# The last stage of a 384-channel attention and binarized-convolution kernel: a written engine order, other queues and 18-partition moves

## Chip, cores and metric

One core of one Trainium2 chip runs the kernel. The metric is device time in microseconds (us) of one execution. The engines are TensorE (PE; its weight loads are PEld), VectorE (DVE), ScalarE (ACT), GpSimd (POOL) and SyncE (SP). DMAs are issued from the queues of SP, ACT and POOL and run on 16 DMA engines.

## The reference

The input x is 1 x 384 x 192 x 192 in float32. Two residual layers follow each other (cut to what matters here):

```python
x = x + L0(gn(x))   # layer 0: channel attention
x = x + L1(gn(x))   # layer 1: binarized 1x1 convolution with shifts

# L0, its end: out is at half resolution
out = gelu(out)
out = repeat(repeat(out, 2, axis=2), 2, axis=3)
out = einsum('bchw,oc->bohw', out, w_proj) + b_proj

# L1
xb = sign(x); wb = sign(weight)
dx = (arange(C) + 3) % 7 - 3          # -3 .. 3, by channel
shifted[:, c, :, w] = xb[:, c, :, w + dx[c]]   # zero outside the row
out = einsum('bchw,oc->bohw', shifted, wb) + bias
```

Only the sign of the normalized x enters layer 1, so its normalization needs the group means and no variance: the kernel takes sign(x - mean).

## The kernel before

The image is cut into 24 units of 8 rows. One unit of x is a tile `xt` of 128 partitions x 3 x 1536 float32 (2304 KB); channel c of the 384 lies at a partition p and a third t that the table `XCH` of `shift_blocks` (L65) gives. Stages 1 to 4 read x for the statistics, for queries and keys, and for the values. At the end of stage 4 the attention output lies in six tiles `chunk`, four units each, in the pool `big`, which has eight buffers; the other two still hold the last two units of x. A short step (L456 to L476) works out `nmean1`, the group means of layer 1.

The **last stage** (L481 to L550) does the rest, unit by unit, from the last unit to the first. For each unit:

- x is in a kept buffer or is loaded (`unit`, L112; L495) through POOL's queue.
- Nine float32 matmuls of 384 columns, each two instructions (L501), give the projection `yps`; six DVE instructions of 768 elements (L510) add it to both rows of each pair in `xt`.
- Three ACT instructions (L516) write the signs as fp8 into one of two tiles `signs`, with rows at a pitch of 196, four of them zero, so that a shift of up to three columns reads zeros beyond a row.
- 14 DMAs through SP's queue (L526) copy the signs to one of two tiles `moved`, each channel shifted by its own dx. Seven of them move 16 partitions with all three thirds (4700 bytes of each partition); six move 7 partitions of one third; one moves 2 partitions.
- 27 fp8 matmuls of 512 columns (L534), in blocks of 4 x 128 or 8 x 64 pixels, give the convolution `l1ps`, one PSUM bank for each block; nine DVE instructions of 512 elements (L542) add it and the bias to `xt`.
- `xt` is stored through POOL's queue (L550).

The order of the instructions on each engine is worked out by the framework's scheduler from dependencies and its own estimates. A buffer for a load comes from `big` or from the pool `more` of two. After every fourth unit a `chunk` has been used up, and its buffer becomes one more for loads. On POOL's queue a load that waits for its buffer stands ahead of later stores.

The functions that the change touches:

Of the kernel before, what the change touches and what calls it, by code (L numbers as in the profile page):

```python
# [10 lines left out]
F32 = mybir.dt.float32  # L11
F8 = mybir.dt.float8e4
AF = mybir.ActivationFunctionType
ALU = mybir.AluOpType
AX = mybir.AxisListType
PSUM = bass.MemoryType.PSUM

P = 128
C = 384
CT = C // P  # L20
# [7 lines left out]
UR = 8  # L28
NU = H // UR
# [2 lines left out]
PPX = PR * WP  # L32
KS = (HD // 2, HD * 2 // 3, HD * 3 // 4, HD * 4 // 5)
SHIFT = 7
SP = 16
PITCH = W + 4
LEAD = 4
SLEN = UR * PITCH
ABLK = 512
NAB = NPX // ABLK  # L40
UC = 4
CR = UC * PR
CPX = CR * WP
NCH = NU // UC
NST = NU * (UPX // 512) * 6
NBIG = 8
MORE = 2
KEEP = 6
RESIDENT = NBIG - NCH
TOPK = 1  # L50
NSIGNS = 2


BLOCKS = ((0, 4, 0, 128), (4, 4, 0, 128), (0, 8, 128, 64))
# [10 lines left out]
def shift_blocks():  # L65

    left = [list(range(s, C, SHIFT)) for s in range(SHIFT)]
    at = np.full((P, CT), -1)  # L70
    blocks = []

    def put(s, p0, n, t0, nt):
        for t in range(t0, t0 + nt):
            for p in range(p0, p0 + n):
                at[p, t] = left[s].pop(0)
        blocks.append((p0, n, t0, nt, (s + SHIFT // 2) % SHIFT - SHIFT // 2))

    for s in range(SHIFT):
        put(s, SP * s, SP, 0, CT)  # L80
    rest = SP * SHIFT
    n = len(left[0])
    for s in range(2 * CT):
        put(s, rest + (s % 2) * n, n, s // 2, 1)
    put(SHIFT - 1, rest + 2 * n, P - rest - 2 * n, 0, CT)
    assert not any(left) and (at >= 0).all()
    return at, blocks


XCH, SHIFTS = shift_blocks()  # L90


@with_exitstack
def conv_preact_kernel(ctx: ExitStack, tc: tile.TileContext, a: dict, out: bass.AP):
    nc = tc.nc
    xv = a["x"].rearrange("u p (t n) -> u p t n", n=UPX)
    ov = out.rearrange("u p (t n) -> u p t n", n=UPX)
# [4 lines left out]
    big = ctx.enter_context(tc.tile_pool(name="big", bufs=NBIG))  # L102
# [4 lines left out]
    bl1 = const.tile([P, CT], F32, name="bl1")  # L107
    nmean0 = const.tile([P, CT], F32, name="nmean0")
    nmean1 = const.tile([P, CT], F32, name="nmean1")
    wb = const.tile([P, CT, C], F8, name="wb")  # L110

    def unit(u, pool=big, queue=nc.sync):  # L112
        xt = pool.tile([P, CT, UPX], F32, name="xt", tag="big")
        queue.dma_start(xt, xv[u])  # L114
        return xt

    def inv_sqrt(pool, y, s, n, tag):
# [43 lines left out]
    kept = {}  # L161
    with tc.tile_pool(name="p1", bufs=1, side="right") as p1, tc.tile_pool(name="p1ps", bufs=2, space=PSUM) as psp:
        stats = p1.tile([P, CT, NST], F32, name="stats0")
        grp = p1.tile([P, CT, C], F32, name="grp_s0")
        for u in reversed(range(NU)):
            xt = unit(u)
# [14 lines left out]
            for t in range(CT):  # L181
                for j in range(UPX // 512):
                    i = (u * (UPX // 512) + j) * 6
# [20 lines left out]
        ps = psp.tile([P, NM], F32, name="bqps")  # L204
        for m in range(NM):
            for t in range(CT):
# [4 lines left out]
                    start=(t == 0),  # L211
                    stop=(t == CT - 1),
# [3 lines left out]
    def padded(pool, n):  # L216


        ts = []
        for m in range(n):  # L220
            t = pool.tile([P, PR + 3, WP + 2], F32, name=f"pooled{m}")
            nc.gpsimd.memset(t, 0.0)
            ts.append(t)
        return ts
# [41 lines left out]
    with tc.tile_pool(name="p2w", bufs=1, side="right") as wp, tc.tile_pool(  # L266
        name="p2t", bufs=2, side="right"
    ) as tp, tc.tile_pool(name="p2qkv", bufs=3, space=PSUM) as pqkv, tc.tile_pool(
        name="p2tr", bufs=2, space=PSUM
    ) as ptr, tc.tile_pool(name="p2g", bufs=1, space=PSUM) as pg:  # L270
        pool = padded(wp, 2 * CT)
        dwo = [wp.tile([P, (PR + 1) * WP], F32, name=f"dw{m}") for m in range(2 * CT)]
        gram = [pg.tile([P, 512], F32, name=f"gram{t}") for t in range(CT)]
        for u in range(NU):
            xt = kept.pop(u) if u in kept else unit(u)
            lo, hi = rows(u)
            n = hi - lo + 1
# [5 lines left out]
            for c0 in range(0, n * WP, P):  # L283
                L = min(P, n * WP - c0)
                qkT = tp.tile([P, 2, C], F32, name="qkT")
                for s in range(2):
                    ps = ptr.tile([P, C], F32, name="tr")
# [3 lines left out]
                first, last = u == 0 and c0 == 0, u == NU - 1 and c0 + P >= n * WP  # L291
                for t in range(CT):
# [4 lines left out]
                        start=first,  # L297
                        stop=last,
# [98 lines left out]
    with ExitStack() as vs:  # L397
# [4 lines left out]
        psp = vs.enter_context(tc.tile_pool(name="p3ps", bufs=2, space=PSUM))  # L402
        pool = padded(wp, CT)
# [3 lines left out]
        todo, steps = [], None  # L407
# [20 lines left out]
        for u in range(NU):  # L428
            xt = unit(u)
# [6 lines left out]
            last = first + hi - lo  # L436
            for m in range(CT):
                parts = []
                for c in range(first // CR, last // CR + 1):
                    r0, r1 = max(first, c * CR), min(last, c * CR + CR - 1)  # L440
# [15 lines left out]
    with tc.tile_pool(name="p5w", bufs=1, side="right") as wp, tc.tile_pool(name="p5mps", bufs=1, space=PSUM) as psp:  # L456
# [5 lines left out]
        ps = psp.tile([P, CT], F32, name="ymps")  # L462
        for m in range(CT):
            for t in range(CT):
# [4 lines left out]
                    start=(t == 0),  # L469
                    stop=(t == CT - 1),  # L470
# [7 lines left out]
    att.close()  # L478


    with tc.tile_pool(name="p5x", bufs=MORE) as more, tc.tile_pool(name="p5s", bufs=1) as sp, tc.tile_pool(  # L481
        name="p5py", bufs=3, space=PSUM
    ) as pyp, tc.tile_pool(name="p5ps", bufs=5, space=PSUM) as psp:
        signs = [sp.tile([P, LEAD + CT * SLEN + PITCH], F8, name=f"signs{i}") for i in range(NSIGNS)]
        moved = [sp.tile([P, CT * SLEN], F8, name=f"moved{i}") for i in range(2)]
        for t in signs:
            nc.gpsimd.memset(t[:, :LEAD], 0.0)
            nc.gpsimd.memset(t[:, LEAD:].rearrange("p (r w) -> p r w", w=PITCH)[:, :, W:], 0.0)  # L488
        free = [big] * RESIDENT + [more] * MORE
        for i, u in enumerate(u for c in reversed(range(NCH)) for u in reversed(range(c * UC, (c + 1) * UC))):  # L490
            if i and i % UC == 0:
                free.insert(0, big)
            pool = free.pop(0)
            free.append(pool)
            xt = kept.pop(u) if u in kept else unit(u, pool, nc.gpsimd)  # L495
            o = chunk[u // UC][:, :, u % UC * PPX : (u % UC + 1) * PPX]
            x5 = xt.rearrange("p t (i a j b) -> p t a i j b", a=2, b=2, j=WP)
            for m in range(CT):
                ps = pyp.tile([P, PPX], F32, name="yps")
                for t in range(CT):  # L500
                    nc.tensor.matmul(  # L501
                        ps,
                        wpr[:, t, m * P : (m + 1) * P],
                        o[:, t, :],
                        start=(t == 0),
                        stop=(t == CT - 1),
                    )
                yb = ps.rearrange("p (i j) -> p i j", j=WP).unsqueeze(3).to_broadcast([P, PR, WP, 2])
                for r in range(2):
                    nc.vector.scalar_tensor_tensor(  # L510
                        x5[:, m, r], yb, bpr[:, m : m + 1], x5[:, m, r], ALU.add, ALU.add
                    )
            sg, mo = signs[i % NSIGNS], moved[i % 2]
            rows3 = sg[:, LEAD : LEAD + CT * SLEN].rearrange("p (t r w) -> p t r w", r=UR, w=PITCH)
            for t in range(CT):
                nc.scalar.activation(  # L516
                    rows3[:, t, :, :W],
                    xt[:, t, :].rearrange("p (r w) -> p r w", w=W),
                    AF.Sign,
                    bias=nmean1[:, t : t + 1],  # L520
                    saturate=False,
                )
            for p0, n, t0, nt, dx in SHIFTS:
                run = nt * SLEN - (PITCH - W)
                at = t0 * SLEN
                nc.sync.dma_start(  # L526
                    mo[p0 : p0 + n, at : at + run], sg[p0 : p0 + n, LEAD + dx + at : LEAD + dx + at + run]
                )
            x4 = xt.rearrange("p t (r w) -> p t r w", w=W)
            for m in range(CT):  # L530
                for r0, nr, c0, ncol in BLOCKS:
                    ps = psp.tile([P, 512], F32, name="l1ps")
                    for t in range(CT):
                        nc.tensor.matmul(  # L534
                            ps,
                            wb[:, t, m * P : (m + 1) * P],
                            mo[:, t * SLEN : (t + 1) * SLEN].rearrange("p (r w) -> p r w", w=PITCH)[:, r0 : r0 + nr, c0 : c0 + ncol],
                            start=(t == 0),
                            stop=(t == CT - 1),
                        )  # L540
                    blk = x4[:, m, r0 : r0 + nr, c0 : c0 + ncol]
                    nc.vector.scalar_tensor_tensor(  # L542
                        blk,
                        ps.rearrange("p (r w) -> p r w", w=ncol),
                        bl1[:, m : m + 1],
                        blk,
                        ALU.add,
                        ALU.add,
                    )
            nc.gpsimd.dma_start(ov[u], xt)  # L550


# [69 lines left out]
```

## Time and profile before

Three runs took 2556.58, 2549.80 and 2550.52 us, median 2550.52. The profiled execution took 2556.03 us; its span, from the first to the last instruction, is 2554.3 us. All durations below come from that one execution.

| what | us | how to read it |
|---|---|---|
| span | 2554.3 | stages 1 to 4 and the short step until about 2113, the last stage from there |
| PE busy | 2247.0 | 88% of the span, 6235 matmuls |
| DVE busy | 1894.8 | 74% |
| ACT busy | 645.0 | 25% |
| L501 matmuls, yps | 166.9 | 432 instructions |
| L534 matmuls, l1ps | 157.3 | 648 instructions |
| L510 adds | 136.3 | 144 instructions, 1011 ns each in the mean |
| L542 adds | 146.0 | 216 instructions, 744 ns each in the mean |
| L516 signs | 108.6 | 72 instructions, 1566 ns each |
| L526 issues of moves | 336 issues | 0.52 to 2.65 us each in SP's queue, median 0.69 |
| x loads, last stage | 22 | 2304 KB each, 10.0 us from issue to landing (median) |
| stores | 24 | 2304 KB each, 10.2 us (median) |

PE's granted clock was full until the last stage and 0.75 to 0.93 in its stretches of 50 us. The DMA engines' share of time was 0.12 in stage 2 and 0.77 to 0.88 in the middle of the last stage.

### The profile page before, as it was taken

How to read it: one execution, taken by the hardware profiler on the slowest of the kernel's cores; microseconds unless marked ns; L12 is line 12 of the kernel's file. 1: busy time of each engine (PE TensorE's matmuls, PEld its weight loads, DVE VectorE, ACT ScalarE, POOL GpSimd, SP SyncE). 2: the span in 40 equal slices, each digit the busy share in tenths (PEclk: the TensorE clock that was granted, in tenths of full speed). 3: DMA queues.
4: the chain of work that ended last, by engine and by line, in shares of the span. 5: the costliest groups of instructions: out<-in, count | busy, mean ns of one | idle time of the engine just before them, and what ended most of it. 6: DMA issues, size and time to landing. Idle time of an engine off the chain costs nothing. (4 is left out here: it accounts for less than half of the span.)

```text
span 2554.3 us, 18523 instructions
## 1 busy us (share of the span) xinstructions
PE 2247.0 (88%) x6235; PEld 1069.3 (42%) x6235; DVE 1894.8 (74%) x3187; ACT 645.0 (25%) x1282; POOL 34.2 (1%) x67
## 2 busy tenths in 40 slices
PE   0039999999999999999999999999999998687864
PEld 0034444444444444444444444444444444343421
DVE  6956777777777777777778899956668676676763
ACT  0002323332322323232322221232222223222131
POOL 0000000000000000000000000000000000000000
PEclk9999999999999999999999999999999999888987
DMA  9941011100110111100100120211011106888976
GB/s 374 430 205 37 37 38 65 47 37 37 54 58 38 37 42 70 37 1 37 37 38 37 65 111 37 111 74 74 37 75 58 71 29 228 301 306 291 331 245 227
DMA packets 28463, 285.25 MB, mean 112 GB/s; under 512 B 8240, under 2 KB 10784, under 8 KB 13904
## 3 DMA queue, kind: packets, MB, share of 16 engines
q1 hardware_dynamic: 16992, 170.17, 18.0%
q0 software_dynamic: 6624, 108.53, 11.0%
q10 hardware_dynamic: 4752, 5.37, 0.6%
q8 instruction: 49, 0.80, 0.1%
q14 instruction: 46, 0.38, 0.0%
HBM read 212.99 MB, written 56.62 MB: 106 GB/s over the span
## 5 line engine op out<-in xcount | busy, mean ns | idle before, releaser
L238 PE MATMUL qkv<-xt,wq 128*128 128x512 f32 x3888 | 1699.4, 593 | 7.7 <-DVE pooled L245 7.4
L238 PEld LDWEIGHTS qkv<-xt,wq 128*128 128x128 f32 x3888 | 727.3, 190 | 871.4 <-issue 798.7
L261 DVE SCALAR_TENSOR_TENSOR dw<-pooled,wdw,dw 128x384 f32<-128x384 f32 (+2 forms) x1152 | 709.5, 616 | 250.9 <-ACT dw L259 226.9
L245 DVE TENSOR_REDUCE pooled<-qkv 128x128 f32<-128x512 f32 x648 | 443.9, 686 | 141.0 <-PE qkv L238 134.1
L261 DVE SCALAR_TENSOR_TENSOR chunk<-pooled,wdw,chunk 128x384 f32<-128x384 f32 (+3 forms) x696 | 362.6, 548 | 46.2 <-ACT chunk L259 34.7
L263 ACT COPY pooled<-pooled 128x196 f32<-128x196 f32 x207 | 73.7, 356 | 737.8 <-DVE dw L261 520.2
L252 ACT ACTIVATE pooled<-pooled,bq 128x384 f32<-128x384 f32 x216 | 133.1, 616 | 386.7 <-DVE pooled L245 386.7
L501 PE MATMUL yps<-chunk,wpr 128*128 128x384 f32 x432 | 166.9, 545 | 68.8 <-DVE xt L510 68.5
L542 DVE SCALAR_TENSOR_TENSOR xt<-l1ps,bl,xt 128x512 f32<-128x512 f32 x216 | 146.0, 744 | 82.8 <-PE l1ps L534 71.8
L534 PE MATMUL l1ps<-moved,wb 128*128 128x512 fp8e4 x648 | 157.3, 402 | 42.4 <-DMA moved<-signs 35.3
L510 DVE SCALAR_TENSOR_TENSOR xt<-yps,bpr,xt 128x768 f32<-128x768 f32 x144 | 136.3, 1011 | 66.8 <-DMA xt<-in_x_dram 51.6
L516 ACT ACTIVATE signs<-xt,nmean 128x1536 fp8e4<-128x1536 f32 x72 | 108.6, 1566 | 301.2 <-DMA moved<-signs 246.9
L501 PEld LDWEIGHTS yps<-chunk,wpr 128*128 128x128 f32 x432 | 90.7, 214 | 139.2 <-DVE xt L510 59.8
L184 DVE BATCH_NORM_STATS2 stats<-xt 128x6 f32<-128x512 f32 x216 | 130.5, 679 | 24.8 <-DMA xt<-in_x_dram 23.8
L133 PE MATMUL gm_m<-cm,grp_s 128*128 128x1 f32 x18 | 4.0, 353 | 161.5 <-DVE cm L189 161.5
L534 PEld LDWEIGHTS <-wb 128*128 128x128 fp8e4 x648 | 65.5, 102 | 134.7 <-issue 54.6
L282 ACT ACTIVATE sq<-dw 128x384 f32<-128x384 f32 (+2 forms) x144 | 75.2, 522 | 157.8 <-DVE dw L261 157.8
L416 PE MATMUL ops<-chunk,aT 128*128 128x512 f32 x252 | 109.0, 592 | 0.0
L259 ACT ACTIVATE dw<-pooled,bdw,wdw 128x384 f32<-128x384 f32 (+2 forms) x144 | 100.8, 700 | 30.0 <-PE tr L289 28.2
L289 PE MATMUL tr<-ident,dw 128*128 128x128 f32 (+2 forms) x438 | 74.2, 279 | 8.8 <-DVE dw L261 8.0
L289 PEld LDWEIGHTS tr<-ident,dw 128*128 128x128 f32 (+2 forms) x438 | 52.3, 140 | 70.4 <-DVE dw L261 30.9
L293 PEld LDWEIGHTS gram<-qkT 128*128 128x128 f32 (+2 forms) x438 | 64.4, 190 | 25.3 <-ACT qkT L290 19.9
(91 smaller groups left out, 470.9 us busy)
## 6 DMA issues: line engine op xcount, KB each, us to landing
xt<-in_x_dram SPq DMA_DIRECT2D x66, 2304.0 KB
out_dram<-xt POOLq DMA_DIRECT2D x24, 2304.0 KB, 10.2
xt<-in_x_dram POOLq DMA_DIRECT2D x22, 2304.0 KB, 10.0
moved<-signs SPq DMA_DIRECT2D x168, 73.4 KB
moved<-signs SPq DMA_DIRECT2D x144, 10.7 KB
wq<-in_w_qkvT_dram ACTq DMA_DIRECT2D x1, 1728.0 KB
grp_s<-in_grp_dram ACTq DMA_DIRECT2D x2, 576.0 KB
tri<-in_tri_dram ACTq DMA_DIRECT2D x1, 1152.0 KB
```

Source lines behind the costliest of these rows:

```text
L184: nc.vector.bn_stats(stats[:, t, i : i + 6], xt[:, t, j * 512 : (j + 1) * 512])
L238: nc.tensor.matmul(ps, wq[:, t, m * P : (m + 1) * P], x4[:, t, r0 : r0 + nr, c0 : c0 + ncol], start=(t == 0), stop=(t == CT - 1),)
L245: nc.vector.tensor_reduce(pl[:, 2 + r0 // 2 : 2 + (r0 + nr) // 2, 1 + c0 // 2 : 1 + (c0 + ncol) // 2], ps.rearrange("p (i a j b) -> p i j ...
L252: nc.scalar.activation(new, new, AF.Identity, bias=bq[:, m : m + 1])
L261: nc.vector.scalar_tensor_tensor(acc2, src, wdw[:, m, k : k + 1], acc2, ALU.mult, ALU.add)
L289: nc.tensor.transpose(ps[:L, t * P : (t + 1) * P], dwo[s * CT + t][:, c0 : c0 + L], ident)
L416: nc.tensor.matmul(ps, aT[:, k, t * P : (t + 1) * P], chunk[c][:, k, cols], start=(k == MEET[t][0]), stop=(k == MEET[t][-1]),)
L501: nc.tensor.matmul(ps, wpr[:, t, m * P : (m + 1) * P], o[:, t, :], start=(t == 0), stop=(t == CT - 1),)
L510: nc.vector.scalar_tensor_tensor(x5[:, m, r], yb, bpr[:, m : m + 1], x5[:, m, r], ALU.add, ALU.add)
L516: nc.scalar.activation(rows3[:, t, :, :W], xt[:, t, :].rearrange("p (r w) -> p r w", w=W), AF.Sign, bias=nmean1[:, t : t + 1], saturate=False,
L534: nc.tensor.matmul(ps, wb[:, t, m * P : (m + 1) * P], mo[:, t * SLEN : (t + 1) * SLEN].rearrange("p (r w) -> p r w", w=PITCH)[:, r0 : r0 + ...
L542: nc.vector.scalar_tensor_tensor(blk, ps.rearrange("p (r w) -> p r w", w=ncol), bl1[:, m : m + 1], blk, ALU.add, ALU.add,)
```

## The change

`shift_blocks` groups 18 partitions per shift instead of 16: seven blocks of 18 partitions with all three thirds, and two left partitions whose thirds need shifts that step by one from third to third, or no shift. A unit then has seven moves of 18 partitions, issued from ACT's queue right after the signs, and three small moves from POOL's queue. The x loads of the last stage go to SP's queue, which carries nothing else there; the stores stay on POOL's.

The last stage is split into two functions. `signed(i)` does the projection, the adds, the signs and the moves of a unit; the signs of a third now follow its adds at once. `finished(i)` does the convolution, the adds of the convolution and the store. They are called in a fixed order, which each engine follows as written: signed(0), then signed(i+1), finished(i) for each i. Loads are issued where a buffer becomes free: after the store of a unit and after the last use of a chunk.

The convolution is cut into 36 matmuls of 384 columns (two image rows each); two of these groups fill two PSUM banks, and one DVE instruction adds 768 elements over both banks, six per unit. The projection has two PSUM buffers instead of three, the convolution three pairs of banks instead of five banks. The last unit is stored in three parts. The pools of the stage are opened with the option that waits for single tiles of what lay in the space before.

```diff
-SP = 16
+SP = P // SHIFT
@@ shift_blocks
-    for s in range(SHIFT):
-        put(s, SP * s, SP, 0, CT)
-    rest = SP * SHIFT
-    n = len(left[0])
-    for s in range(2 * CT):
-        put(s, rest + (s % 2) * n, n, s // 2, 1)
-    put(SHIFT - 1, rest + 2 * n, P - rest - 2 * n, 0, CT)
+    for i, dx in enumerate(sorted(left)):
+        put(i * SP, SP, 0, CT, dx)
+    put(P - 2, 1, 0, CT, 1, 1)
+    put(P - 1, 1, 0, 2, -3, 1)
+    put(P - 1, 1, 2, 1, 0)
@@ last stage
+        def opened(name, bufs, **kw):
+            return last.enter_context(tc.tile_pool(name=name, bufs=bufs, reuse_waits="tile", **kw))
+        more, sp = opened("p5x", MORE), opened("p5s", 1)
+        pyp, psp = opened("p5py", 2, space=PSUM), opened("p5ps", 3, space=PSUM)
...
-        free = [big] * RESIDENT + [more] * MORE
-        for i, u in enumerate(u for c in reversed(range(NCH)) for u in reversed(range(c * UC, (c + 1) * UC))):
-            if i and i % UC == 0:
-                free.insert(0, big)
-            pool = free.pop(0)
-            free.append(pool)
-            xt = kept.pop(u) if u in kept else unit(u, pool, nc.gpsimd)
+        free = [more] * MORE
+        todo = [u for u in order if u not in kept]
+        home = {u: big for u in kept}
+        def loads():
+            while free and todo:
+                u = todo.pop(0)
+                home[u] = free.pop(0)
+                kept[u] = unit(u, home[u])
+        def signed(i):
...
-            for p0, n, t0, nt, dx in SHIFTS:
-                run = nt * SLEN - (PITCH - W)
-                at = t0 * SLEN
-                nc.sync.dma_start(
-                    mo[p0 : p0 + n, at : at + run], sg[p0 : p0 + n, LEAD + dx + at : LEAD + dx + at + run]
-                )
+            for p0, n, t0, nt, dx, step in SHIFTS:
+                at = LEAD + dx + t0 * SLEN
+                if step or nt < CT:
+                    one = SLEN - (PITCH - W)
+                    src = sg[p0 : p0 + n, at : at + nt * (SLEN + step)]
+                    nc.gpsimd.dma_start(
+                        to[p0 : p0 + n, t0 : t0 + nt, :one],
+                        src.rearrange("p (t n) -> p t n", t=nt)[:, :, :one],
+                    )
+                else:
+                    run = CT * SLEN - (PITCH - W)
+                    nc.scalar.dma_start(
+                        to[p0 : p0 + n].rearrange("p t n -> p (t n)")[:, :run], sg[p0 : p0 + n, at : at + run]
+                    )
+            if i % UC == UC - 1:
+                free.append(big)
+                loads()
+        def finished(i):
...
             for m in range(CT):
-                for r0, nr, c0, ncol in BLOCKS:
-                    ps = psp.tile([P, 512], F32, name="l1ps")
-                    for t in range(CT):
...
-                    blk = x4[:, m, r0 : r0 + nr, c0 : c0 + ncol]
+                for r0 in range(0, UR, 4):
+                    ps = psp.tile([P, 2, 512], F32, name="l1ps")
+                    for j in range(2):
+                        for t in range(CT):
+                            nc.tensor.matmul(
+                                ps[:, j, : 2 * W],
+                                wb[:, t, m * P : (m + 1) * P],
+                                mo[:, t, r0 + 2 * j : r0 + 2 * j + 2, :W],
+                                start=(t == 0),
+                                stop=(t == CT - 1),
+                            )
+                    blk = xt[:, m, r0 * W : (r0 + 4) * W].rearrange("p (j n) -> p j n", j=2)
                     nc.vector.scalar_tensor_tensor(
...
+                        blk, ps[:, :, : 2 * W], bl1[:, m : m + 1], blk, ALU.add, ALU.add
+                    )
+                if i == NU - 1:
+                    nc.gpsimd.dma_start(ov[u, :, m], xt[:, m])
+            if i < NU - 1:
+                nc.gpsimd.dma_start(ov[u], xt)
+            free.append(home[u])
+            loads()
+        with tc.manual_schedule():
+            loads()
+            signed(0)
+            for i in range(NU):
+                if i < NU - 1:
+                    signed(i + 1)
+                finished(i)
```

## The prediction

> **What bounds the kernel now.** I read the table of stretches first, to find the last stage and its engines. The stage starts with the first yps matmul at 2112.9 us and ends with the span, so it is 441 us of 2554.3. The stores are the milestones: the first was issued at 2149.1, the 16th at 2441.7, the 24th at 2544.4. The last x load was issued at 2433.9. That cuts the stage into four: 36 us of start, 15 store intervals of 19.5 us with loads running (292.6 us), 8 intervals of 12.8 us without loads (102.7 us), 9.9 us of end.
>
> ```profile
> 2149.00:2441.00 292.00, 222.52 (x745) 112.11 (x744) 196.70 (x249) 66.16 (x45) 18.06 (x34) 0.87 0.84 306
> 2441.00:2544.00 103.00, 60.85 (x223) 23.81 (x221) 55.31 (x79) 27.05 (x18) 4.26 (x8) 0.78 0.68 226
> ...
> 2262.00:2270.00 8.00, 3.11 (x10) 1.53 (x9) 6.05 (x8) 1.49 (x2) 0.54 (x1) 0.80 1.01 380
> ...
> 2398.00:2406.00 8.00, 7.58 (x33) 3.35 (x31) 6.78 (x10) 0.00 (x0) 0.47 (x1) 1.00 0.99 378
> ```
>
> The columns are PE, PEld, DVE, ACT and POOL busy, then granted clock, DMA share, GB/s. With loads running, PE is busy 76%, DVE 67%, and the DMA engines 84% at 306 GB/s. Seven 8 us stretches in which the share reached 0.97 to 1.04 moved 356 to 401 GB/s, 380 in the mean. So no engine is full, but DMA has only a fifth to give. What keeps them all from being full shows in the waits of that stretch (total us, times, longest) and in the chain of waits (start, us, what).
>
> ```profile
> ACT signs L516 <- DMA moved<-signs: 200.4, 13, 23.5
> POOL xt L114 <- DMA out_dram<-xt: 164.6, 14, 17.5
> ...
> DVE xt L510 <- DMA xt<-in_x_dram: 49.3, 12, 8.2
> ```
>
> ```profile
> 2229.00 10.12 DMA out_dram<-xt
> ...
> 2239.67 9.69 DMA xt<-in_x_dram
> ...
> 2249.48 1.95 DVE xt L510 x2
> ...
> 2264.68 15.67 DMA out_dram<-xt
> ```
>
> The loop is: store, load into its buffer, residual add of that load, PE behind the add (yps waited 68.5 us for L510's buffers), next store. The load issued at 2239.7, when the fifth store had landed, is the eleventh unit's; its add sits in DVE's and PE's order ahead of the l1ps work of the sixth unit. The order runs five units ahead, so finished work waits for a load that waits for a store. The loop takes some 36 to 40 us and passes two units. Without loads the limit is another one: SyncE's queue, which issues moves without a pause. The timeline (start, us, engine, line; in brackets the idle time before and its releaser) has it last, under the prices of a unit's l1ps work on PE and DVE:
>
> ```profile
> 2198.25 5.99 PE L534 MATMUL l1ps<-moved,wb 128*128 128x512 fp8e4 x27
> ...
> 2199.17 6.02 DVE L542 SCALAR_TENSOR_TENSOR xt<-l1ps,bl,xt 128x512 f32<-128x512 f32 x9 [4.87 <-PE l1ps L534]
> ...
> 2440.51 95.14 SPq L526 DMA_DIRECT2D moved<-signs  x98
> ```
>
> 98 issues in 95.1 us, 14 per unit, is 13.6 us per unit against the interval of 12.8 in those units. PE and DVE need 6.0 us each for one unit's l1ps and are idle for the rest.
>
> **The change, step by step.** Call S the work of `signed` and F that of `finished`.
>
> *Prices per unit.* PE: S is unchanged, 18 matmuls in 6.07 us where it runs at full clock (2150.8). F has 36 matmuls of 384 columns for 27 of 512, the same 13,824 columns. No row has an fp8 matmul of 384, so it lies between 5.99 us (by columns) and 8.0 us (36 at the 0.222 us of each of the 27). I take 6.0, because the f32 matmuls of 384 and 512 columns go by columns: 0.337 us (6.07/18) against 0.437 (1699.4/3888). PE is then 12.1 us. DVE: F has six adds of 768 elements instead of nine of 512; at the 0.94 us of L510 (six in 5.64 from 2188.7) that is 5.64 instead of 6.02, so DVE is 11.3 us. The 0.4 us saved is worth nothing, since PE covers it; without that cover it would be 9 us in all. Two yps buffers instead of three cost nothing while DVE empties one (1.9 us) as fast as PE fills the other (2.0); a late DVE would hold PE by 1.9 us per unit. ACT: 4.5 us of signs as now, plus seven issues that were SyncE's. An undisturbed issue took 0.59 us (2482.9); seven under traffic, from 2440.5, took 0.55, 0.90, 0.58, 1.59, 1.40, 1.74 and 2.35, together 9.1. ACT is 8.6 to 13.6 us. Behind a blocked issue stand the next unit's signs, and behind them its moves. POOL: three small moves and a store at 0.53 us, 2.1 us. The small moves stand in POOL's queue behind the store of unit i-1, which took 10 to 16 us to land; F of i+1 needs them an interval and an S later (17 + 6 us by the sum below), so they cost nothing, but a store over 23 us would show. SyncE: loads alone, each waiting only for its buffer; nothing stands behind them but later loads.
>
> *The moves on the DMA engines.* Bytes stay at 0.60 MB per unit, but 18 partitions replace 16. These are the queue totals of the 292 us, and then q1 on the page (packets, MB, share of 16 engines):
>
> ```profile
> q0 software_dynamic: 4874, 80.11, 72.6%
> q1 hardware_dynamic: 4659, 9.01, 11.6%
> ```
>
> ```profile
> q1 hardware_dynamic: 16992, 170.17, 18.0%
> ```
>
> The page's 16,992 packets are 66 loads of 128+16 and 24 units of 7x(16+16) + 6x(7+7) + (2+2): one data packet and one closing packet per partition of a move, so 16 partitions used 16 engines. 18 on 16 engines put two on at least one, so the fullest engine gets 14 big packets per unit where an even spread would give 7.9. A 4.7 KB packet costs 0.28 us (11.6% of 292 x 16 engine-us is 542 for 9.01 MB). The surplus is between 0 (that engine catches up in lulls) and 6.1 x 0.28 = 1.7 us per unit, 26 us over 15 units. The rows do not say which, so I take the middle, 13. The Trainium skill (DMA: Bandwidth & Descriptors, "Why a DMA increments its semaphore by 16 and not by 1") states that a DMA uses the largest number of engines up to 16 that divides the slowest dimension, which for 18 would be nine engines with two each. The counts for 16 and 7 agree with it, no row shows 18; by it the 26 would hold and the end would be 13 us later.
>
> *Start.* The signs of the first unit ended at 2124.4 and still will. Seven issues of 0.59 (4.1) and 2.4 us of landing (2471.9) give 2130.9; F with its last add 6.9. The first store comes at 2138 instead of 2149.1, because F of the first unit no longer stands behind S of the fourth. 11 us gained. The first two loads may now start before 2113.7; I cost that at nothing, since S of the third unit comes only after 2137, when they have landed (10 us) even if issued as now.
>
> *The 15 intervals with loads.* A load now has all the buffers' slack, S is one unit ahead, so the loop above opens and the DMA engines become the bound. Work between first and 16th store, if the loads again run ahead: 15 stores, 20 loads, 15 units of moves, 35 x 2.36 + 9.0 = 91.6 MB. At 380 GB/s that is 241 us, with the surplus 254, 16.9 us per unit. PE (12.1), DVE (11.3) and ACT (13.6 at worst) lie beside it. Bounds: 241 to 267.
>
> *The 8 intervals without loads.* SyncE's 13.6 us of issues are gone; PE's 12.1 is next, 97 us instead of 102.7. DMA needs 5.3 us for a store (2.36 MB at the 442 GB/s of 2546 to 2550) and at most 3.9 of moves. If F costs 8.0, it is 113.
>
> *End.* The last unit is stored in thirds, so only a third follows the last add: 9.9 - 2/3 x 5.3 = 6.4 us.
>
> *Sum.* 2138 + 254 + 97 + 6.4 = 2495 us of span, 59 less than 2554.3. The profiled execution took 2556.0, 1.7 more than its span; the median of the three is 2550.5, 5.5 below it. 2495 + 1.7 - 5.5 is **2491** us.
>
> **Rivals.**
>
> *ACT blocked by its own issues (slower).* The place is ACT's queue; the price is issue time under three busy queues with two packets on one engine. If all seven took the 2.35 us of the worst above, ACT would need 16.5 + 4.5 = 21 us per unit: 2138 + 315 + 8 x 13.6 + 6 is 2568, at 2564 in the median's terms. At the longest issue seen, 2.65, it is 23 us and 2595. It decides from about 2.2 us per issue on, where 15 intervals reach 20.1 us. For it: every long issue in the trace falls in bulk traffic. Against it: the mean was 1.0. The same page ("Queues, rings and completion order") says that an engine takes turns among its queues packet by packet. By that rule 14 packets, each behind one load and one store packet of 0.78 us (72.6% of 292 x 16, over 4333 data packets), would last an estimated 26 us if both queues were never empty; no run here shows three busy queues.
>
> *Loads that do not run ahead (faster).* If loads spread over the whole stage, all 44 transfers and 13.9 MB of moves at 380 GB/s take 310 us, with no unit left that PE alone sets: 2138 + 310 + 6 is 2454, 2450 in the median. Against it: stores come one per unit, and SyncE's loads take whatever is left.
>
> *The loop stays (no change).* If each load still meets its add just in time, because stores (10.1), loads (9.7), S with its signs (7.4), moves (6.5) and F (6.9) are a 41 us loop passing two units, the interval is 20.3: 2138 + 305 + 97 + 6 is 2546, 2542 in the median. Against it: at least four buffers, later up to nine, would pass four or more.
>
> **How the numbers follow.** The forecast, 2465 to 2535, has 0.57; ACT blocked 0.20; loads spread 0.15; the loop stays 0.08. What can be told from no change is 0.3%, 7.7 us: faster is below 2542.9. The staying loop lies on that line; a fourth of it counts as faster, the rest as the same. So faster is 0.57 + 0.15 + 0.02 = 0.74, the same 0.06, slower 0.20. The range goes from 2445, just under the spread loads, to 2565, with the cheaper half of the blocked ACT inside.
>
> **What would show it.** Right: a first store near 2138; intervals near 17 us with DMA share at 0.95 or more until the last load; then intervals near 12 with PE over 90% busy; the adds of L510 no longer waiting for loads. Wrong in size: fp8 matmuls of 384 columns at 0.22 us each. The blocked ACT would show as issues over 2 us each in ACT's queue, and l1ps matmuls waiting for moves with the DMA share below 0.9. The forecast falls if the intervals stay over 19 us.

## The result and the profile after

The changed kernel takes 2566.84 us (median of four runs, 2564.17 to 2570.66) against 2551.43 us of the kernel before in the same comparison: a ratio of 1.0058, 95% interval 1.0036 to 1.008. It is 0.6% slower. The forecast was 2491 us with a range up to 2565, so it was wrong in sign, and the time lies just above the range.

The profiled execution took 2564.17 us, with a span of 2562.3. Its stores cut the stage as before:

| term | before | forecast | after | after minus forecast |
|---|---|---|---|---|
| first store at | 2149.1 | 2138 | 2142.4 | +4.4 |
| 15 intervals with loads | 292.5 | 254 | 282.6 | +28.6 |
| the last 8 intervals | 102.7 | 97 | 127.9 | +30.9 |
| end | 9.9 | 6.4 | 9.4 | +3.0 |
| span | 2554.3 | 2495 | 2562.3 | +67 |

(The last eight intervals of after end with the issue of its last third.) Against before, the start gained 6.7 us and the intervals with loads 9.9; the last eight lost 25.2. The first reading is the table of stretches of after, cut at the same milestones (window and length, then PE, PEld, DVE, ACT and POOL busy, granted clock, DMA share, GB/s):

```profile
2142.00:2425.00 283.00, 197.11 (x812) 107.01 (x812) 173.53 (x181) 70.22 (x45) 31.48 (x61) 0.86 0.85 314
2425.00:2553.00 128.00, 94.46 (x410) 51.64 (x408) 86.50 (x90) 33.09 (x21) 16.40 (x32) 0.89 0.59 214
```

With loads running, PE is busy 70% and DMA has a share of 0.85 at 314 GB/s; before it was 76%, 0.84 and 306. So DMA did not become the bound. Without loads DMA is at 0.59 and PE at 74%, where the forecast wanted PE over 90%. Something else holds both stretches. The waits from 2100 to the end (total us, times, longest) name it:

```profile
ACT signs L524 <- DVE xt L521: 269.8, 60, 20.4
...
POOL out_dram L573 <- DVE xt L567: 164.3, 23, 16.2
...
DVE xt L567 <- PE l1ps L559: 131.9, 31, 16.2
PE l1ps L559 <- DMA moved<-signs: 115.0, 12, 16.0
```

Read from below: PE waited 115 us in 12 places for moves; DVE waited behind PE, the store on POOL behind DVE, and ACT's signs for the adds that stand behind in DVE's order. The line of before that had the x adds wait for loads is gone. The timeline shows what one such wait is made of (start, us; in brackets the idle time before and its releaser):

```profile
2150.88 10.18 ACTq L543 DMA_DIRECT2D moved<-signs  x7
...
2157.36 2.17 PE L512 MATMUL yps<-chunk,wpr 128*128 128x384 f32 x6 [0.19 <-DVE xt L521]
...
2165.78 9.64 ACTq L543 DMA_DIRECT2D moved<-signs  x7
...
2173.91 8.16 PE L559 MATMUL l1ps<-moved,wb 128*128 128x384 fp8e4 x36 [14.37 <-DMA moved<-signs]
...
2188.13 6.21 PE L559 MATMUL l1ps<-moved,wb 128*128 128x384 fp8e4 x36
```

The moves of one unit are issued from 2150.88 on. PE has finished the next unit's S at 2159.53 and, by the written order, may do nothing but this unit's F; that begins at 2173.91. So the moves needed **23.0 us**, from the first issue to F, and the order gives them 8.7. In this unit 4.9 of the 23.0 passed in ACT's queue: the seventh issue stood from 2155.5 to 2160.3, until an x load had landed (why is told at e7). But the sixth move, which had not stood, landed only at 2170.7 by the counts of its semaphore, so most of the wait is slow landing. The three small moves on POOL's queue had landed by 2160.8. Meanwhile the next unit's moves, issued at 2165.8, arrive too, so the F at 2188.1 waits for nothing. That is why the stores come in pairs: 12.7 us apart, then 14 to 30.

The same without loads, from the chain of waits (start, us, what) and its neighbours:

```profile
2461.68 1.95 PE yps L512 x6
...
2469.93 1.58 ACT signs L524
2471.53 0.74 ACTq L543
...
2475.40 0.73 ACTq L543
2476.17 8.20 DMA moved<-signs
2484.37 0.39 issue
2484.77 7.69 PE l1ps L559 x36
2492.46 1.95 PE yps L512 x6
```

S begins at 2461.5, its moves are issued from 2471.5 on, 10.0 us later, and F begins 13.2 us after that. The packet records in the trace show how the last move came to take 8.2 us: the first six moves' 108 packets had ended by 2478, some 20 to 25 a microsecond; a store issued at 2475.7 moved its packets from 2477 to 2484, and the 18 packets of the seventh move ended among them, the last at 2483 to 2484.

Call m the time from a unit's first issue to its F. Two units then take 10.0 + m + F. For the two shown it gives 10.0 + 23.0 + 8.2 = 41.2 and 10.0 + 13.2 + 7.7 = 30.9; the stores were 41.0 (2142.4 to 2183.4) and 30.8 us apart (2475.7 to 2506.5). Up to m = 8.7 the moves are hidden, and above it each microsecond costs half a microsecond per unit.

The wait has a second price. In the stretch just after the 14.4 us of idle, PE's granted clock was 0.50:

```profile
2174.00:2176.00 2.00, 2.00 (x7) 0.89 (x7) 0.00 (x0) 0.00 (x0) 0.00 (x0) 0.50 1.03 335
```

The twelve F behind a wait for moves, of 4.0 to 16.0 us, took 7.3 to 9.0 us; the others took 6.0 to 6.2, one of them after 3.9 us of idle.

### The profile page after: what moved, and what is told of

It is laid out like the page before. It is cut to its first block, busy times and chain, and to the rows that moved or that the text cites. A ratio compares the mean times of both kernels' runs of the same rounds, so it can differ in the third digit from the quotient of the medians.

```text
span 2562.3 us, 18696 instructions
## 1 busy us (share of the span) xinstructions
PE 2242.7 (88%) x6451; PEld 1084.0 (42%) x6451; DVE 1890.3 (74%) x3115; ACT 649.2 (25%) x1282; POOL 61.2 (2%) x119
## 5 line engine op out<-in xcount | busy, mean ns | idle before, releaser
L559 PE MATMUL l1ps<-moved,wb 128*128 128x384 fp8e4 x864 | 169.6, 360 | 119.2 <-DMA moved<-signs 115.0
L567 DVE SCALAR_TENSOR_TENSOR xt<-l1ps,bl,xt 128x768 f32<-128x768 f32 x144 | 138.8, 1011 | 132.9 <-PE l1ps L559 131.9
L559 PEld LDWEIGHTS <-wb 128*128 128x128 fp8e4 x864 | 90.9, 106 | 201.3 <-issue 156.9
L512 PE MATMUL yps<-chunk,wpr 128*128 128x384 f32 x432 | 151.5, 496 | 4.2 <-DVE xt L521 4.2
L181 DVE BATCH_NORM_STATS2 stats<-xt 128x6 f32<-128x512 f32 x216 | 130.4, 678 | 25.5 <-DMA xt<-in_x_dram 24.7
L256 ACT ACTIVATE dw<-pooled,bdw,wdw 128x384 f32<-128x384 f32 (+2 forms) x144 | 100.8, 700 | 30.0 <-PE tr L286 28.1
L512 PEld LDWEIGHTS yps<-chunk,wpr 128*128 128x128 f32 x432 | 80.4, 192 | 66.2 <-PE yps L512 17.1
```

The costliest lines, as they stand in the source:

```text
L181: nc.vector.bn_stats(stats[:, t, i : i + 6], xt[:, t, j * 512 : (j + 1) * 512])
L512: nc.tensor.matmul(ps, wpr[:, t, m * P : (m + 1) * P], o[:, t, :], start=(t == 0), stop=(t == CT - 1),)
L559: nc.tensor.matmul(ps[:, j, : 2 * W], wb[:, t, m * P : (m + 1) * P], mo[:, t, r0 + 2 * j : r0 + 2 * j + 2, :W], start=(t == 0), stop=(t == ...
L567: nc.vector.scalar_tensor_tensor(blk, ps[:, :, : 2 * W], bl1[:, m : m + 1], blk, ALU.add, ALU.add)
```

## The experiments

In all kernels below the seven moves copy the same bytes seen as uint8. That alone (e0) is the base of the comparisons: 2563.37 us, ratio to before 1.0045 (1.0030 to 1.0061).

> The changed kernel with one difference: the seven big moves name their bytes as uint8 instead of fp8. All later experiments are made from this one. Every theory expects the changed kernel's time, 2567 us (2560 to 2573), with its pairs of store intervals, about 13 and 22 to 29 us.

**No moves at all (e1).** What do the moves and the waits for them cost together?

```diff
-            for p0, n, t0, nt, dx, step in SHIFTS:
...
+        for t in moved:
+            nc.gpsimd.memset(t, 0.0)
```

> All sign moves are left out (the convolution reads tiles of zeros, so its part of the output is not computed from the signs). It shows what the stage takes without moves and their waits. Theory A (moves land late, and the written order leaves them some 10 us, so TensorE stands) expects even intervals of 12.4 to 13 us: 2131 + 23 x 12.7 + 6, about 2430 us. Theory B (the DMA engines are full, the order does not matter): loads and stores alone are 35 x 5.3 us between the first and the 16th store, so also about 2430. Over 2480 us would mean that neither names the bound and that loads, stores or TensorE hold the stage by themselves.

Measured: 2422.02 us, ratio 0.9489 (0.9474 to 0.9505), 141 us below e0. Its stretch with loads:

```profile
2149.00:2350.00 201.00, 197.19 (x882) 111.40 (x882) 186.00 (x198) 78.68 (x50) 8.51 (x16) 1.00 1.00 417
```

PE is busy 98% at full clock, the stores come every 12.28 us, and DMA moves 417 GB/s. Order, adds, loads and stores alone are as fast as the forecast had S and F; nothing but the moves keeps the stage from PE's 12.1 us per unit. It also shows that 380 GB/s, on which the forecast's 254 us stood, was no ceiling of DMA. But the share is 1.00 here without the bytes of the moves, so the run doesn't show that a stage with moves could keep 12.3 us per unit while loads run, nor how the 141 us divide between the moves' bytes and the waits for them.

**S and moves two units ahead, first try (e2).**

```diff
+            signed(1)
             for i in range(NU):
-                if i < NU - 1:
-                    signed(i + 1)
+                if i < NU - 2:
+                    signed(i + 2)
                 finished(i)
```

> Order alone: signed(i+2) in front of finished(i), the two tiles of signs and moves kept. A move then has finished, signed and signed of other units (18 us) between its issue and its use, instead of finished and signed less the signs (some 10 us). Theory A expects intervals of about 16 us with loads (DMA engines full) and under 13 us without, about 2490 us (2465 to 2515). Theory B expects no gain, 2555 to 2570 us. Theory C (loads and moves hinder each other in the hardware queues) expects a part of it, about 2520 us.

Measured: 2811.91 us, ratio 1.1020 (1.1003 to 1.1037). The expectation missed by 320 us, and the fault is the experiment's. There are two `moved` tiles, so the moves of unit i+2 go into the tile that F of unit i is still to read: F(i) uses the signs of unit i+2, and it waits for moves that were issued just ahead of it. The miss is still a measurement, of a stage in which no move is hidden. The waits of PE:

```profile
PE l1ps L561 <- DMA moved<-signs: 337.7, 22, 21.2
```

22 waits of 15.4 us in the mean, and store intervals of some 30 us with loads and 25 us without.

**Loads off SyncE's queue (e3).** The loads go to POOL, where the stores are, the small moves to SyncE.

```diff
-                kept[u] = unit(u, home[u])
+                kept[u] = unit(u, home[u], nc.gpsimd)
...
-                    nc.gpsimd.dma_start(
+                    nc.sync.dma_start(
```

> The loads go back to POOL's queue, beside the stores, and the three small moves go to SyncE's queue, so that they do not stand behind a waiting load; big moves stay on ACT's. Theory C (a move issued after a load stands behind it in the hardware queues and shares its eight semaphores) expects the long intervals of each pair to shrink by the 5 to 8 us that moves were delayed behind loads, about 2490 to 2510 us. Theory A alone expects moves still behind stores, 2535 to 2555 us. Theory B expects 2567 us.

Measured: 2557.72 us (ten runs), ratio 1.0028 (1.0013 to 1.0042). The interval overlaps e0's, and the time lies between the expected ranges. It isn't a clean test of the loads' queue, though. In the changed kernel single moves stood in ACT's queue for loads, 29.9 us in six places (gaps of over 0.3 us between the issues of a unit); here none does, but single moves stand 63.8 us in 24 places for earlier moves, since the small moves now take part in the same eight semaphores (see e7).

**Moves of 16 partitions again (e4).** The order stays; `SP = 16` and the old layout bring back seven moves of 16 partitions on ACT and seven small ones on POOL.

```diff
-SP = P // SHIFT
+SP = 16
...
+    for s in range(2 * CT):
+        put(s, rest + (s % 2) * n, n, s // 2, 1)
...
-                if step or nt < CT:
+                if n < SP:
```

> The 18-partition layout alone is undone: seven moves of 16 partitions on ACT's queue, and the six of 7 and the one of 2 partitions on POOL's. A big move then puts one packet on each of 16 engines instead of two on each of nine. Theory A1 (the lateness is the second packet's turn on the nine engines: 14 packets behind loads and stores instead of 7) expects the waits of l1ps for moves to fall from 115 us to about half, 2510 to 2535 us. Theory A2 (a move waits for whole loads and stores in front of it, however its packets are spread) expects 2555 to 2567 us.

Measured: 2529.15 us, ratio 0.9917 (0.9900 to 0.9935), 34 us below e0. The stages of its profile are 2138.0, 269.0 and 109.8 us. PE still waits for moves, but less:

```profile
PE l1ps L564 <- DMA moved<-signs: 79.2, 10, 11.8
```

The timeline near the end shows that without loads they can be on time:

```profile
2449.65 4.36 ACTq L547 DMA_DIRECT2D moved<-signs  x7
...
2458.15 6.21 PE L564 MATMUL l1ps<-moved,wb 128*128 128x384 fp8e4 x36
```

Seven issues take 4.4 us instead of 5.4, and F follows 8.5 us after the first of them with no wait, so units are 12.3 us apart (2453.9, 2466.1, 2478.4). The page of after shows how 16 and 18 differ:

```profile
q10 hardware_dynamic: 9288, 19.59, 2.5%
```

The queue had 4752 packets before, so the 168 big moves added 4536, which is 27 each: 18 of data and 9 closing ones. In the old layout a move of 16 partitions had 16 and 16. So 18 partitions go to nine engines, two on each. This agrees with the Trainium skill (DMA: Bandwidth & Descriptors, "Why a DMA increments its semaphore by 16 and not by 1"), by which a DMA takes the largest number of engines up to 16 that divides the slowest dimension. How much of the 34 us comes from the spread over engines, and how much from the shorter issues, was not separated.

**The scheduler's order with everything else new (e5), and with 16 partitions too (e13).**

```diff
-        with tc.manual_schedule():
+        with ExitStack():
```

> The written order alone is undone: the framework's scheduler orders the last stage, with the queues, moves and adds of the changed kernel. If the written order with one unit of slack is what gives the change's gain away, the scheduler's order, which runs several units ahead, should be faster than 2563 us: 2500 to 2540. If moves are late for any order, or the scheduler's order again lets adds wait for loads as before, 2550 to 2600 us.

> Both undone at once: the scheduler's order (e5_scheduler, 2534 us) and 16-partition moves (e4_sixteen, 2529 us); queues and adds as in the changed kernel. If the two are separate losses of some 30 us, 2495 to 2505 us. If both are the same lateness of moves, met by an order with more slack or by faster moves, 2520 to 2532 us.

Measured: e5 2533.78 us (eight runs), ratio 0.9935 (0.9916 to 0.9953); e13 2536.08 us, ratio 0.9933 (0.9913 to 0.9953). The written order costs 30 us against e0. The stages of e5's profile are 2146.0, 282.2 and 93.8 us: no gain over after with loads, 34 us in the last eight intervals. Its last projection ends at 2446.5, as before's did (2443), while after's ends at 2527. The scheduler does the S of the last units while loads hold the stage back; the written order, one unit ahead, leaves seven of them for the end, with the waits for moves between them. With that order the layout makes no difference (e13 lies 4 us above the range expected if both undo the same loss). Sixteen partitions and a freer order remove the same thing, the lateness of the moves, so their 34 and 30 us do not add up.

**A written order with more room for the moves (e7, e8).** S goes two units ahead, and the moves are split off into `shifted(i)`, issued as soon as F has read their tile. The moves now have S, F and S of other units, some 18 us, in front of their F.

```diff
-            signed(0)
+            for i in range(2):
+                signed(i)
+                shifted(i)
             for i in range(NU):
-                if i < NU - 1:
-                    signed(i + 1)
+                if i < NU - 2:
+                    signed(i + 2)
                 finished(i)
+                if i < NU - 2:
+                    shifted(i + 2)
```

> Two units ahead, with the moves of unit i+2 issued after the matmuls of finished(i), which free their tile: signed(i+2), finished(i), moves(i+2). (In e2_two_ahead these moves stood before finished(i), which so used signs of another unit and waited for moves just issued: its 2812 us show the whole time of a move, with no slack at all.) A move now has signed, finished and signed of other units, 18 us, until its use. Theory A expects intervals of 15 to 16 us with loads and under 13 us without, 2470 to 2500 us. Theory B (nothing but less DMA work helps) expects 2555 to 2570 us.

> e7_two_ahead with the 16-partition layout of e4_sixteen. If lateness is all hidden by two units, the layout matters only through the work of the fullest engine: seven packets of 4.7 KB less on it, 2 us per unit while loads run, 20 to 30 us under e7_two_ahead. If the layout matters not at all, equal to e7_two_ahead within 5 us.

Measured: e7 2531.70 us, ratio 0.9917 (0.9901 to 0.9933); e8, with 16 partitions, 2522.45 us, ratio 0.9887 (0.9871 to 0.9902). e7 gains 32 us, and meets a wait that the expectation had not priced; 16 partitions are worth 9 us here, less than the 20 to 30 expected of the fullest engine and more than the 5 of no effect. From e7's timeline:

```profile
2204.34 29.57 ACTq L551 DMA_DIRECT2D moved<-signs  x7
...
2234.09 4.50 ACT L525 ACTIVATE signs<-xt,nmean 128x1536 fp8e4<-128x1536 f32 x3 [29.78 <-DMA xt<-in_x_dram]
```

Seven issues last 29.6 us, and what released ACT at the end is an x load. In four units the seventh move stood 8 to 25 us in ACT's queue for a load that it has no data in common with. The program counts the DMAs of SyncE's and ACT's queues on the same eight semaphores (100 to 107 in the trace) in turn, and an issue waits until the DMA counted before on its semaphore has landed. So a move that gets a load's semaphore waits for the load. After has it too, at its units 3, 7, 11 and 16, with 4.9 to 8.6 us.

**The same with the loads on POOL (e9, 18 partitions; e10, 16); and 16 partitions one ahead with loads on POOL (e11).** These join the edits shown for e7, e3 and e4.

> The same as e10_two_ahead_sixteen_pool with the 18-partition layout of the change: e7_two_ahead with the loads on POOL's queue. Theory C expects it well under e7_two_ahead's 2532 us, 2485 to 2515. Theory A1 (packets on the fullest of the engines) expects 20 to 30 us more than e10_two_ahead_sixteen_pool; if the layout is harmless once moves have slack, within 5 us of it.

> e8_two_ahead_sixteen with the loads on POOL's queue and the seven small moves on SyncE's, so that loads and big moves no longer take turns on the same eight semaphores of the hardware queues. In e7_two_ahead the last big move of units 3, 7, 11 and 15 stood 8, 20, 25 and 22 us in ACT's queue until a load had landed. Theory C (that wait is what two units ahead still lose) expects it gone and intervals of 14 to 15 us with loads, 12.4 without: 2465 to 2490 us. If the remaining waits for moves come from the DMA engines being full, as at 0.93 of their time in e8_two_ahead_sixteen, little changes: 2510 to 2522 us.

> e4_sixteen (one unit ahead, moves of 16 partitions) with the loads on POOL's queue and the small moves on SyncE's. In e3_loads_pool that step gave 6 us. If load and move hinder each other through shared semaphores mainly at the chunk ends, where e4_sixteen stood 4.6 to 10.4 us six times, it gives some 20 us: 2505 to 2515 us. If lateness behind bulk packets is all, 2522 to 2530 us.

Measured: e9 2507.25 us, ratio 0.9819 (0.9803 to 0.9836); e10 2511.58 us, ratio 0.9831 (0.9807 to 0.9854); e11 2526.72 us, ratio 0.9897 (0.9880 to 0.9914). e9 is the best of all, 1.8% below the kernel before, and within its expected 2485 to 2515; e10 missed the 2465 to 2490 expected if the loads' semaphores were all that was left. Moving the loads, worth little with one unit ahead (e3, and e11 against e4), is worth 24 us once the order gives room. Between e9 and e10, 18 partitions are no worse than 16. In e9 PE's waits for moves have shrunk, and two other waits have grown:

```profile
ACT signs L525 <- DMA moved<-signs: 218.6, 20, 15.8
POOL xt L112 <- DMA out_dram<-xt: 196.9, 11, 24.3
...
PE l1ps L565 <- DMA moved<-signs: 46.1, 12, 7.1
```

The first is ACT held back by its own queue, as the timeline shows:

```profile
2217.53 13.43 ACTq L551 DMA_DIRECT2D moved<-signs  x7
...
2231.09 4.51 ACT L525 ACTIVATE signs<-xt,nmean 128x1536 fp8e4<-128x1536 f32 x3 [13.58 <-DMA moved<-signs]
```

The seven issues end at 2230.96, and the signs start 0.1 us later; in the other units too they start within 0.4 us of the last issue. The issues take so long because ten moves of a unit now go round the eight semaphores: single moves stand 100.8 us in 42 places for earlier moves, and none for a load. The second is the old price of POOL's queue:

```profile
2227.53 0.53 POOL L112 DMA_DIRECT2D xt<-in_x_dram  x1 [17.19 <-DMA out_dram<-xt]
2228.06 0.54 POOL L579 DMA_DIRECT2D out_dram<-xt  x1
```

A load that waits for its buffer's store stands in front of the next store. Which of the two sets e9's remaining time was not separated.

**The moves on POOL as well (e12).** Order of e7, loads on SyncE, but all moves from POOL.

```diff
-                    nc.scalar.dma_start(
+                    nc.gpsimd.dma_start(
```

> e7_two_ahead (loads on SyncE's queue) with all ten moves on POOL's queue, after the store. The hardware queues then carry loads alone, and POOL's queue has no waiting load in front of stores, as it has in e9_two_ahead_pool, where store intervals were 17 to 18 us. If those two queue effects are what still keeps the DMA engines from being full, intervals of 15 to 16 us with loads: 2475 to 2495 us. If moves on POOL wait for each other and for stores (11 transfers of a unit on POOL's semaphores), 2505 to 2540 us.

Measured: 2523.91 us, ratio 0.9880 (0.9861 to 0.9898). The first of the expected ranges, 2475 to 2495, is missed. The move no longer waits for a load; on POOL it waits for stores and for other moves instead:

```profile
POOL moved L545 <- DMA out_dram<-xt: 133.3, 22, 11.3
...
POOL moved L551 <- DMA moved<-signs: 71.2, 47, 3.1
```

**One bank per add again (e14).** The old blocks of 512 columns, nine adds per unit.

> The step on the convolution's adds alone is undone: 27 matmuls of 512 columns and nine adds of 512 elements per unit, one bank each, five banks, and three yps buffers. TensorE needs 6.0 instead of 6.2 us for it, VectorE 6.0 instead of 5.6. While TensorE waits for moves, either is worth nothing: 2558 to 2568 us, as e0_bytes. If the pairs of banks or the two yps buffers hold TensorE up, 2545 to 2555.

Measured: 2556.95 us (ten runs), ratio 1.0016 (1.0000 to 1.0031); the time lies between the two expected ranges, and its interval touches e0's. So the adds over two banks have no clear part in the loss.

## Why the prediction was wrong

**The step that failed** is the price of the moves: "Seven issues of 0.59 (4.1) and 2.4 us of landing". The 2.4 us came from a move with little beside it (in the trace of before it is the first move of the next unit, of 16 partitions, issued at 2471.85), and the 6.5 us were then taken as hidden under PE in every interval. In after, m is 13.2 and 23.0 us in the two units shown; over the units whose F waited, it is 8.2 in the first, with little traffic beside it, and 12.5 to 24.7 beside stores and loads. The forecast never asked how much room the written order leaves. It leaves 8.7 us. The forecast's own terms would have given 10.8: F's 6.0 and the next S's 6.1, less the 1.3 by which its 7.4 for S with the signs exceeds S (after shows 10.0 for S with the signs). That is room for 6.5 us of moves, and none for a move that waits out a store of 10. The prediction listed a late move only inside the rival of the blocked ACT, and there as issue time.

**Start, 2138.** Measured 2142.4. The landing was right (2.3 us). Issues took 6.0 us instead of 4.1, and F 8.2 instead of 6.0, since PE came out of a wait.

**Intervals with loads, 254 us bound by DMA.** Measured 282.6, and not bound by DMA: share 0.85, while e1 reached 417 GB/s at a share of 1.00. By the rule of two units, 282.6 / 7.5 = 37.7 us is a mean m near 20. The surplus of 18 partitions was looked for on a full engine; its place was the lateness, and the layout was worth 34 us with one unit ahead (e4), and with two 9 us (e7 and e8) or nothing that can be told (e9 and e10).

**Intervals without loads, 97 us.** Measured 127.9. PE's 12.1 us per unit is right as a floor (e1's 12.28, e4's 12.3), but m stayed above 8.7 without loads too, since each store lies over the moves of the unit behind it. Here the change lost to before: before's last eight intervals contained F alone, as its PE busy of 60.9 us in 103 showed. The prediction saw 13.6 us of SyncE's issues in them and the change as a gain; it did put S back into these intervals, but not the wait that comes with it.

**End, 6.4.** Measured 9.4. A third landed 3.6 us after its issue (median of the three), but 5.8 us follow the last; what fills them is not known.

**Offset.** The forecast subtracted 5.5 us, by which before's profiled run lay above its median. After's lies 2.7 below its own. That is 8 of the 76 us between forecast and median; the four terms above are the other 67.

**What was right.** F's 36 matmuls of 384 columns go by columns: 6.01 to 6.21 us. Adds of 768 elements took 0.94 us. The adds no longer wait for loads, so the loop of before is open (e1 shows that the loads keep up). Nine engines for 18 partitions, as counted.

**The rivals.** The sign of "ACT blocked by its own issues" came true, and its time (2564) is near, but by luck: its price, long issues, did not occur. Its mark was issues of over 2 us; the line of the issues says otherwise (min/median/max ns):

```profile
L543 ACTq DMA_DIRECT2D moved<-signs x168: 728/736/1422, 2124.6 to 2536.0; - x168
```

ACT needs 5.4 us for seven of them. What did block ACT's queue in part are the waits between the issues, for loads (29.9 us in all) and for earlier moves (9.1 us): with them a unit's moves took 7.1 us of the queue on average, against the 16.5 of the rival's sum. The other mark it shared with the truth: l1ps matmuls waiting for moves with the DMA share below 0.9. The Trainium skill's rule quoted there (DMA: Bandwidth & Descriptors, "Queues, rings and completion order", an engine takes turns packet by packet) gave an estimate of 26 us for a unit's moves beside two busy queues. That was put down to the issues; as landing time it would have been nearer to the measured m than 6.5 is, but no run here shows the turns. The loads did not spread over the whole stage (the last was issued at 2434.6, against 2433.9 before), and the loop did not stay.

**What stays open.** Whether the packets of a move are late because engines take turns with the bulk queues, or because of what the transfers share at their ends, no run separates. Nor does a run separate how much of the loss the waits for a load's semaphore make: e3 and e9 put waits for earlier moves in their place.

## What to carry to other kernels

Before fixing an order by hand, write down for each transfer that sits between two engines the time from its first issue to its use, priced beside the traffic that will run then, and compare it with the work that the order places between; one unit ahead gave 8.7 us to moves that need 12.5 to 24.7 beside traffic. Count in that time what an issue waits for in its queue, a shared semaphore too. When a queue or an order is freed, look at what the old order had done in advance (here the S of the last seven units) and count it again. A wait for a transfer on the busiest engine is paid twice where the clock falls in the wait.

## What was not expected of the hardware

- Small moves beside bulk traffic: the last move of after's first unit, with little beside it, was used 3.0 us after its issue (2129.8 to 2132.8); a move under one store of 2304 KB took 8.2 us, and a unit's moves up to 24.7 us from first issue to use beside a store and loads.
- PE after 14.4 us of idle ran at a granted clock of 0.50 for 2 us; 36 matmuls took 8.2 us instead of 6.2.
- Loads and stores together reached 417 GB/s over 200 us with no moves between them, above the 356 to 401 of before's fullest stretches.
- An issue of a move of 18 partitions takes 0.74 us in ACT's queue, one of 16 partitions about 0.60.
